# Attention without transposes: sums and values sent round by DMA, values of a half batch together, exponentials of two PSUM banks in one instruction

## The chip, the cores and the metric

The kernel runs on one core of a Trainium2 chip. Five engines work side by side: TensorE (matmuls and transposes), VectorE, ScalarE, GpSimd, and SyncE, which issues most of the DMAs. Each takes its own instructions in the order in which the program lists them. The metric is the device time of the core in microseconds. TensorE's granted clock in the profiled execution was 0.998 of full speed.

## The reference

Two layers on eight sequences of 256 tokens with 256 features, all in float32. Each layer is a residual attention and a residual feed-forward part, behind a layer norm:

```python
x = x + L0_xattn(layernorm(x), ctx, ctx, ...)   # correlation by FFT, the 12 best shifts
x = x + L0_ffn(layernorm(x), ...)               # tokens dealt out to 8 experts of equal load
x = x + L1_xattn(layernorm(x), ctx, ...)        # softmax attention: what the change touches
x = x + L1_ffn(layernorm(x), ...)               # top 2 of 8 experts, and a shared expert
```

The third line, cut to what matters:

```python
q = (x @ Wq + bq).reshape(bs, n_ctx, 16, 16)
kv = (data @ Wkv + bkv).reshape(bs, n_data, 16, 32)
k, v = kv[..., :16], kv[..., 16:]
attn = softmax(einsum('bqhd,bkhd->bhqk', q, k) / 4)
out = einsum('bhqk,bkhd->bqhd', attn, v).reshape(bs, n_ctx, 256)
return out @ Wp + bp
```

There are 16 heads of 16 features, and 256 queries and 256 keys in each of the eight batches. The softmax divides by the sum of the exponentials; the kernel makes the products with the undivided exponentials and divides their result.

## The kernel before, in words

`fast_path` holds the whole program. Its stages follow each other on TensorE: the first layer up to some 213 us, the attention of the second layer from there to 348 us, and the second feed-forward part after that, whose first matmuls (`classic_up`, the shared expert on the first 512 tokens) fill TensorE while the attention's last batch is finished.

The attention runs over `b` (8 batches) and, inside, `c` (2 halves of the heads, 8 heads each). The order of work is written out by hand in that loop: what is called there is what the engines' queues hold, in that order.

- `scores(b, c, kt)`: for one of two key tiles `kt` (128 keys), four matmuls over 32 rows of the array each (two heads per 32 rows, of which a mask keeps one at a time apart), into four PSUM banks of the pool `ps_s`; then ScalarE's exponentials from PSUM into `ex` in SBUF (L2652, L2660).
- `values(b, c, m)`: the exponentials times the values `VA`. Each head has a group of 32 columns: 16 for its features, and a further one that gives the sum of the exponentials (row `DH` of each 32). Two heads m sit beside each other in one PSUM bank of `ps_v` (L2667). It needs the exponentials of both key tiles, so it is called one step late, for the (b, c) before, named `prev`.
- `keep` copies that bank to SBUF as `ov` (L2677, VectorE).
- `turn_back(b)`: transposes `ov` on TensorE, so that queries lie on partitions, takes the reciprocal of the sums (`rs`) and multiplies (L2687, L2694, L2695). `turn_out(b)` transposes the result back (L2706), and VectorE copies it to `oT` (L2712).
- `project_out(b)`: `oT` times `wp`, added to `X` (L2718, L2726).
- Around it, for other batches: `add_y` (the first layer's result added to `X`), `batch_stats` and `batch_norm` (mean and variance on VectorE, a Newton step on GpSimd, the normalisation on VectorE and GpSimd by halves: `norm_q`, tile `h`; and for the next layer `norm_m`, tile `HP`), `turn_q` (transposes `h`, VectorE copies to `hT`), `queries` (`QM` by ScalarE and then VectorE), `turn_m` (transposes `HP`, ScalarE copies to `HT`), `add_bias` on GpSimd.
- `route(g)` is a generator for 4 tiles of 128 tokens: it chooses the experts in eight small steps over TensorE, VectorE and ScalarE, and leaves 8 rows of work in `sends`; `send()` issues one as an indirect DMA from GpSimd into `Td`. The first experts' rows `R` are loaded from `Td` once all are there (L3491).

PSUM has eight banks: three for `ps_m` (everything with a transpose or a projection), four for `ps_s`, one for `ps_v`. After the loop, a tail written out by hand ends the last two batches and the routes 2 and 3 between steps of `classic_up`, which uses `ps_s` for its products (`pgt`, `pu`), as does `first_down`.

## Time and profile before

| what | value |
|---|---|
| median of the runs | 833.5 us (the runs: 832.12, 833.5, 1887.65) |
| the profiled execution | 830.43 us, span 828.7 us |
| TensorE busy | 806.3 us, 97% of the span |
| VectorE busy | 522.3 us, 63% |
| ScalarE busy | 348.7 us, 42% |
| GpSimd busy | 216.8 us, 26% |
| attention loop, first scores to last values | 223.00 to 347.78 us |

One execution is recorded. A group's line gives source line, engine, operation, what is written and read, the count, busy time and mean duration in ns, then the idle time before it and what ended it. A busy TensorE isn't one at its peak: matmuls are pipelined and their ends are modelled, so in a timeline the distance from start to start says more than the length. In a window's line stand its length, the busy time of each engine with the count of instructions, the granted clock, the DMA engines' busy share and GB/s. The chain of waits is followed back from the last instruction to what released each step. The run of 1887.65 stands alone, and nothing below rests on it.

### The profile page before, as it was taken

How to read it: one execution, taken by the hardware profiler on the slowest of the kernel's cores; microseconds unless marked ns; L12 is line 12 of the kernel's file. 1: busy time of each engine (PE TensorE's matmuls, PEld its weight loads, DVE VectorE, ACT ScalarE, POOL GpSimd, SP SyncE). 2: the span in 40 equal slices, each digit the busy share in tenths (PEclk: the TensorE clock that was granted, in tenths of full speed). 3: DMA queues.
4: the chain of work that ended last, by engine and by line, in shares of the span. 5: the costliest groups of instructions: out<-in, count | busy, mean ns of one | idle time of the engine just before them, and what ended most of it. 6: DMA issues, size and time to landing. Idle time of an engine off the chain costs nothing.

```text
span 828.7 us, 13872 instructions
## 1 busy us (share of the span) xinstructions
PE 806.3 (97%) x5188; PEld 636.2 (77%) x5188; DVE 522.3 (63%) x1470; ACT 348.7 (42%) x720; POOL 216.8 (26%) x293
## 2 busy tenths in 40 slices
PE   7999999999999999999999999999999999999997
PEld 6546787778745555557898989797979798999996
DVE  6377877440456586555775866767676758586731
ACT  4344454324377777431333233333333433443430
POOL 6251131230125455452330000202111232112020
PEclk9999999999999999999999999999999999999999
DMA  8395567942160000042120474656575754311023
GB/s 261 97 277 177 178 207 224 297 158 84 51 178 15 14 1 28 34 168 89 67 67 26 142 242 135 190 168 187 172 199 161 201 167 122 105 13 20 8 35 124
DMA packets 87316, 105.40 MB, mean 127 GB/s; under 512 B 9000, under 2 KB 77832, under 8 KB 87208
## 3 DMA queue, kind: packets, MB, share of 16 engines
q1 hardware_dynamic: 78568, 91.10, 35.0%
q0 software_dynamic: 7920, 13.02, 7.2%
q8 instruction: 43, 0.70, 0.4%
q10 hardware_dynamic: 752, 0.30, 0.1%
q14 instruction: 33, 0.27, 0.1%
HBM read 80.61 MB, written 25.37 MB: 128 GB/s over the span
## 4 chain that ended last, share of the span: by engine, by line
PE 88%; DMA 5%; DVE 3%; POOL 2%; ACT 1%; issue 1%; ACTq 0%; SPq 0%; DVEq 0%; POOLq 0%
PE a L3234 18%; PE e L3234 9%; PE a L3293 9%; PE py L2389 6%; PE ph L2372 5%; PE B L3234 5%; PE e L3293 4%; PE p L2652 4%; PE py L3439 3%; PE pv L2667 3%; PE B L3293 2%; PE pp L2718 2%; DMA R<-NMd,ids 2%; PE pgt L3196 2%; PE pp L2619 2%; PE pu L3196 2%
## 5 line engine op out<-in xcount | busy, mean ns | idle before, releaser
L3518 POOL DMA_INDIRECT Od<-Y,ids x32 | 51.6, 1612 | 300.5 <-DVE T L3083 184.0
L3222 ACT COPY B<-a 128x512 f32<-128x512 f32 (+1 forms) x54 | 28.6, 531 | 180.5 <-PE a L3234 142.6
L2660 ACT ACTIVATE ex<-p,scale 128x512 f32<-128x512 f32 x128 | 77.2, 689 | 27.5 <-PE p L2652 26.3
L3234 PE MATMUL a<-T,HP 128*128 128x256 f32 x288 | 73.9, 379 | 0.0
L3083 DVE TENSOR_TENSOR cc<-e,s 128x512 f32<-128x512 f32 x44 | 30.4, 691 | 58.0 <-PE e L3234 58.0
L3234 PE MATMUL a<-RT,wab 128*128 128x256 f32 x256 | 66.6, 383 | 0.0
L3083 DVE TENSOR_TENSOR act<-act 128x256 f32<-128x256 f32 (+1 forms) x120 | 61.4, 512 | 2.7
L2372 PE MATMUL ph<-RT,w 128*128 128x256 f32 x256 | 61.7, 389 | 0.8 <-ACT RT L2359 0.7
L2389 PE MATMUL py<-w,A 128*128 128x256 f32 x256 | 61.6, 388 | 0.0
L3234 PEld LDWEIGHTS a<-T,HP 128*128 128x128 f32 x288 | 54.0, 190 | 7.0
L3234 PEld LDWEIGHTS a<-RT,wab 128*128 128x128 f32 x256 | 46.4, 190 | 8.4 <-issue 1.6
L2381 ACT ACTIVATE A<-ph,b1c 128x256 f32<-128x256 f32 x64 | 30.0, 472 | 53.9 <-PE ph L2372 50.6
L2372 PEld LDWEIGHTS ph<-RT,w 128*128 128x128 f32 x256 | 45.3, 190 | 8.9 <-ACT A L2381 1.1
L2389 PEld LDWEIGHTS py<-w,A 128*128 128x128 f32 x256 | 46.6, 190 | 6.4
L2892 POOL DMA_INDIRECT Td<-HP,to x32 | 32.9, 1030 | 56.9 <-DMA Td<-HP,to 51.6
L2652 PE MATMUL p<-QM,KT 32*128 32x512 f32 x256 | 43.4, 640 | 0.4 <-DVE QM L2633 0.4
L3083 DVE TENSOR_TENSOR act<-act,cc 128x512 f32<-128x512 f32 x44 | 30.4, 691 | 17.6 <-ACT act L3268 17.1
L2399 POOL DMA_INDIRECT Yd<-Y,ids x16 | 15.7, 984 | 81.9 <-DVE Y L2398 49.0
L2667 PE MATMUL pv<-ex,VA 128*32 128x256 f32 x512 | 34.5, 385 | 0.2 <-DVE ov L2677 0.2
L3249 ACT COPY s<-a 128x512 f32<-128x512 f32 x44 | 25.7, 585 | 20.4 <-PE a L3234 20.4
L2667 PEld LDWEIGHTS pv<-ex,VA 128*32 128x32 f32 x512 | 13.5, 109 | 27.0 <-issue 11.7
L3234 PE MATMUL e<-T,wab 128*128 128x256 f32 x128 | 33.0, 380 | 0.3 <-DVE T L3083 0.3
(525 smaller groups left out, 1745.0 us busy)
## 6 DMA issues: line engine op xcount, KB each, us to landing
w<-in_L_ffn_w_dram SPq DMA_DIRECT2D x16, 1024.0 KB, 6.0
wab<-in_L_ffn_w_e_dram SPq DMA_DIRECT2D x16, 1024.0 KB, 4.9
wc<-in_L_ffn_w_e_dram SPq DMA_DIRECT2D x8, 1024.0 KB, 5.4
sab<-in_L_ffn_w_e_dram SPq DMA_DIRECT2D x32, 256.0 KB, 2.9
R<-Td SPq DMA_DIRECT2D x8, 530.0 KB, 3.7
sc<-in_L_ffn_w_e_dram SPq DMA_DIRECT2D x16, 256.0 KB, 2.8
Td<-blank SPq DMA_DIRECT2D x2, 1590.0 KB, 10.2
X<-in_x_dram SPq DMA_DIRECT2D x4, 512.0 KB, 5.3
```

Of the source, the lines that this page charges most:

```text
L2372: nc.tensor.matmul(ph, w1[:, kc, f * P : (f + 1) * P], RT[:, kc, :], start=(kc == 0), stop=(kc == KC - 1),)
L2381: nc.scalar.activation(A[:, f, :], ph, AF.Gelu_apprx_tanh, bias=b1c[:, e, f : f + 1])
L2389: nc.tensor.matmul(py, A[:, f, r * P : (r + 1) * P], w2[:, f, :], start=(f == 0), stop=(f == NF - 1),)
L2652: nc.tensor.matmul(ps[g].rearrange("p m q -> p (m q)"), KT[rows, c, k0 : k0 + P], QM[b][rows, c].rearrange("p m q -> p (m q)"), start=True ...
L2660: nc.scalar.activation(e4[:, g], ps[g], AF.Exp, scale=scale)
L2667: nc.tensor.matmul(pvs[b, c][32 * g : 32 * g + 32, m, :], VA[:, b * TPB + kt, 8 * c + 2 * g + m, :], ex[b, c, kt][:, g, m, :], start=(kt = ...
L2892: nc.gpsimd.indirect_dma_start(out=Td, out_offset=bass.IndirectOffsetOnAxis(ap=to[g][:, k, j : j + 1], axis=0), in_=HP[:, GT * g + j, :], ...
L3083: eng.tensor_tensor(out, a, b, op)
L3196: nc.tensor.matmul(ps, wab[:, m, kc, fs], xs[kc], start=(kc == 0), stop=(kc == KC - 1),)
L3234: nc.tensor.matmul(ps[:, m * HT2 : (m + 1) * HT2], self.w.get(m, left, self.k), self.x.part[right], start=start and m == 0, stop=True, ski ...
L3293: nc.tensor.matmul(ps[:, qs], self.acts[k][:, left, qs], self.w.get(right, k), start=start and i == 0 and k == 0, stop=(k == NK - 1), skip ...
L3518: nc.gpsimd.indirect_dma_start(out=Od, out_offset=bass.IndirectOffsetOnAxis(ap=ids, axis=0), in_=Y, in_offset=None, compute_op=ALU.add,)
```

## The change

- **No transposes for the division.** `turn_back` and `turn_out` are gone. `keep` now also sends the rows of sums from `ov` by DMA to a tile `rs` of 128 partitions with 16 sums each, and the whole of `ov` to a DRAM tile `VD`. `factors`, called after the next scores, takes the reciprocal of `rs` on VectorE, stores it to DRAM (`FD`), and loads two tiles: `num`, the values in the layout that `project_out` wants, from `VD`; and `fac`, the factors repeated over the 16 features of each head, from `FD`. `scaled_values`, a step later, multiplies them into `oT`.
- **Values of a half batch in one go.** Both `values` calls and `keep` follow directly on the first `scores` of a step.
- **Exponentials of two banks at once.** `ps_s` has two buffers of two banks; one instruction takes 1024 elements per partition. `classic_up` and `first_down` use the same two-bank tiles.
- **The loop's order.** `project_out`, the statistics and `norm_m` of a batch, and the routes, come a batch earlier. The shared expert's weights are loaded by `load_shared`, one DMA at the end of each of six steps, instead of all at the end of the first. The tail follows suit.

The core of the diff:

```diff
-    ps_s = banks.enter_context(tc.tile_pool(name="ps_s", bufs=4, space=PSUM))
+    ps_s = banks.enter_context(tc.tile_pool(name="ps_s", bufs=2, space=PSUM))
...
-        ps = [ps_s.tile([P, 2, S], F32, tag="p", name=f"p{g}") for g in range(4)]
+        ps = [ps_s.tile([P, 2, 2, S], F32, tag="p", name=f"p{j}") for j in range(2)]
...
-        for g in range(4):
-            nc.scalar.activation(e4[:, g], ps[g], AF.Exp, scale=scale)
+        for j in range(2):
+            nc.scalar.activation(
+                e4[:, 2 * j : 2 * j + 2], ps[j], AF.Exp, scale=scale
+            )
...
     def keep(b, c):
-        ovs[b, c] = pxs.tile([P, 2, S], F32, tag="ov", name="ov", bufs=3)
-        nc.vector.tensor_copy(ovs[b, c], pvs.pop((b, c)))
-
-    def turn_back(b):
...
-    def turn_out(b):
...
+        ov = pxs.tile([P, 2, S], F32, tag="ov", name="ov")
+        nc.vector.tensor_copy(ov, pvs.pop((b, c)))
+        rs = pxs.tile([P, 16], F32, tag="rs", name="rs")
+        nc.sync.dma_start(
+            out=rs, in_=ov[DH::32].rearrange("g m (y e) -> g (m y) e", e=16)
+        )
+        VD = dram.tile([P, 2, S], F32, name=f"VD{b}_{c}")
+        nc.sync.dma_start(out=VD, in_=ov)
+        parts[b, c] = VD, rs
+
+    def factors(b, c):
+        VD, rs = parts[b, c]
+        rr = pxs.tile([P, 16], F32, tag="rr", name="rr")
+        nc.vector.reciprocal(rr, rs)
+        FD = dram.tile([4, 2, S], F32, name=f"FD{b}_{c}")
+        nc.sync.dma_start(
+            out=FD.rearrange("g m (y e) -> (g m y) e", e=16), in_=rr
+        )
+        num = pxs.tile([P, S], F32, tag="num", name="num")
+        fac = pxs.tile([P, S], F32, tag="fac", name="fac")
+        half = [slice(m * P // 2, (m + 1) * P // 2) for m in range(2)]
+        for m in range(2):
+            nc.sync.dma_start(
+                out=num[half[m]],
+                in_=VD.rearrange("(g w) m q -> g w m q", g=4)[:, 0:DH, m],
+            )
+        for m in range(2):
+            nc.sync.dma_start(
+                out=fac[half[m]],
+                in_=FD[:, m].unsqueeze(1).to_broadcast([4, DH, S]),
+            )
+        parts[b, c] = num, fac
+
+    def scaled_values(b, c):
+        num, fac = parts.pop((b, c))
+        if c == 0:
+            oTs[b] = pxs.tile([P, NB, S], F32, tag="oT", name="oT")
+        nc.vector.tensor_tensor(oTs[b][:, c, :], num, fac, ALU.mult)
...
+    def load_shared(wab, wc):
+
+        for m, w in enumerate((L1_ffn_w1_s, L1_ffn_w3_s)):
+            for kc in range(KC):
+                nc.sync.dma_start(
+                    out=wab[:, m, kc, :].rearrange("p (n f) -> p n f", f=P),
+                    in_=w[:, kc * P : (kc + 1) * P, :].rearrange("n p f -> p n f"),
+                )
+                yield
+        w = L1_ffn_w2_s.rearrange("n p d -> p n d")
+        for h in range(2):
+            ns = slice(h * NF // 2, (h + 1) * NF // 2)
+            nc.sync.dma_start(out=wc[:, ns, :], in_=w[:, ns, :])
+            yield
```

The loop after the change, one step (b, c), with what holds for the first step alone left out:

```python
            scores(b, c, 0)
            if before:
                values(*before[-1], 0)
                values(*before[-1], 1)
                keep(*before[-1])
...
            if c == 1 and b + 2 < B:
                norm_q(b + 2, nc.vector, nc.vector if b < 2 else nc.gpsimd)
                add_bias(b + 2)
            gate()
            send()
            scores(b, c, 1)
            if before:
                factors(*before[-1])
            gate()
...
            elif c == 0:
                if b + 1 < B:
                    queries(b + 1, 0)
                    queries(b + 1, 1)
                if b >= 1:
                    scaled_values(*before[-2])
                if b >= 2:
                    turn_m(b - 2)
                if b + 2 < B:
                    add_y(b + 2)
                    batch_stats(b + 2, "q")
            else:
                if b + 2 < B:
                    turn_q(b + 2)
                if b >= 1:
                    scaled_values(*before[-2])
                    project_out(b - 1)
                    batch_stats(b - 1, "m")
                    norm_m(b - 1)
            if c == 0 and b >= 3 and b % 2:
                gates.append(route(b // 2 - 1))
            gate()
            send()
            if before:
                next(shared_loads, None)
```

`gate()` takes one step of the oldest open route. In `classic_up` and `first_down`:

```diff
-                pgt = ps_s.tile([P, TB], F32, tag="p", name="pgt")
-                pu = ps_s.tile([P, TB], F32, tag="p", name="pu")
...
+                pgu = ps_s.tile([P, 2, TB], F32, tag="p", name="pgu")
...
-        pys = [ps_s.tile([P, D], F32, tag="p", name="py") for _ in range(FULL)]
...
+        for r in range(FULL // 2):
+            two = ps_s.tile([P, 2, TB], F32, tag="p", name="py")
```

The tail after the loop:

```python
    last = before[-1]
    values(*last, 0)
    values(*last, 1)
    keep(*last)
    scaled_values(*before[-2])
...
    factors(*last)
    gate()
...
    next(up0)
    gate()
    next(up0)
    turn_m(B - 2)
    gate(len(gates) * 8)
    send(4)
    scaled_values(*last)
    next(up0)
    project_out(B - 1)
    batch_stats(B - 1, "m")
    norm_m(B - 1)
    send(len(sends))
    next(up0)
    next(up0)
    turn_m(B - 1)
```

## The prediction

> **What bounds the kernel now.** I read the page first, to see which engine is busy; then TensorE's timeline, to find where the attention loop begins and ends; then busy time by batch; and last the chain of waits in order of time.
>
> The page, busy time and two groups of the attention loop:
>
> ```profile
> PE 806.3 (97%) x5188; PEld 636.2 (77%) x5188; DVE 522.3 (63%) x1470; ACT 348.7 (42%) x720; POOL 216.8 (26%) x293
> ...
> L2660 ACT ACTIVATE ex<-p,scale 128x512 f32<-128x512 f32 x128 | 77.2, 689 | 27.5 <-PE p L2652 26.3
> ```
>
> TensorE hardly rests, and the exponentials wait for it (26.3 us), not it for them. The change lies in the loop that runs from the first scores at 223.00 us to the last values at 347.78 us. Busy time by stretch, one batch b per line (b = 2, 3, 4, 6):
>
> ```profile
> core 0: us, PE busy (x) PEld busy (x) DVE busy (x) ACT busy (x) POOL busy (x), PEclk, DMA share, GB/s
> ...
> 251.33:266.49 15.16, 14.92 (x133) 8.00 (x133) 9.48 (x24) 11.28 (x19) 8.53 (x15) 1.00 0.07 19
> 266.49:281.69 15.20, 14.97 (x135) 8.28 (x134) 9.99 (x31) 11.29 (x19) 8.33 (x15) 1.00 0.07 19
> 281.69:297.86 16.17, 15.38 (x151) 8.43 (x150) 10.50 (x31) 11.03 (x20) 9.03 (x15) 1.00 0.01 3
> ...
> 313.56:328.52 14.96, 14.96 (x146) 8.09 (x145) 7.87 (x25) 10.54 (x20) 8.90 (x12) 1.00 0.08 28
> ```
>
> A plain batch takes 15.2 us, TensorE is busy for 15.0 of it, and the DMA engines are nearly idle. All eight take 14.0, 14.3, 15.2, 15.2, 16.2, 15.7, 15.0 and 19.3, 124.8 in sum. In TensorE's timeline of b = 3, with the start, the length and the count:
>
> ```profile
> 274.53 1.14 PE L2652 MATMUL p<-QM,KT 32*128 32x512 f32 x8
> 275.61 1.07 PE L2667 MATMUL pv<-ex,VA 128*32 128x256 f32 x16
> 276.61 1.09 PE L2687 MATMUL pt<-ident,ov 128*128 128x128 f32 x8
> 277.54 0.60 PE L2605 MATMUL pt<-ident,HP 128*128 128x128 f32 x4
> ```
>
> From start to start: scores 1.08, half the values 1.00, `turn_back` 0.93, `turn_m` 0.53. Eight matmuls of `project_out` or `queries` take 1.92 from start to start here, but 1.72 in the tail (360.38 to 362.10), where they follow matmuls of the same shape: each change of shape costs some 0.15 to 0.2.
>
> A full TensorE can still be fed late. The chain of waits for the same batch (start, length, what):
>
> ```profile
> 272.68 1.94 PE pp L2619 x8
> 274.64 0.57 ACT QM L2626
> 275.24 0.54 DVE QM L2633
> 275.78 0.61 DVE X L2553
> ...
> 279.81 1.37 POOL h L2581
> 281.22 0.55 PE pt L2605 x3
> ```
>
> From `queries` over ScalarE, VectorE (`QM`, `add_y`, statistics) and GpSimd (Newton step, half of `norm_q`) to `turn_q`, 8.5 us in all. TensorE has just enough other work between the two and loses a quarter of a us. **The change brings these two ends closer together.**
>
> **What the skill says.** "ScalarE: Activation LUTs", section "What ACT_TABLE_LOAD costs": 0.833 ns an element, and successive instructions overlap by about 93 ns. The trace agrees: one exponential of 512 takes 0.69, four in a row 2.42. "DMA: Bandwidth & Descriptors", section "Anatomy of one DMA": a fixed part of about 2 us whatever the size; here `ids_s<-ids_p` of 0.1 KB lands after 1.8, `yg` of 256 KB after 2.6. The same page, "Why a DMA increments its semaphore by 16": a transfer uses as many DMA engines as divide the slowest dimension of both sides; four for `rs`, `num` and `fac`, whose slowest dimension is g. No run shows that yet. "PSUM — Partial Sum Buffer", section "Engine vs sequencer instructions": ScalarE and VectorE are strict FIFO, so a VectorE instruction that waits for a DMA holds all behind it.
>
> **The change, part by part.**
>
> *Transposes.* 64 in `turn_back` and 32 in `turn_out` go: from start to start 0.9 and 0.5 a batch, 11.4 us for eight, all on TensorE's path (1.3 of it in the tail). On VectorE two reciprocals (0.25), two products (0.42) and the `oT` copy (0.68) go, 2.0 a batch; two reciprocals of 128x16 (bounds 0.18 to 0.25, from the rows of 128x4 and of 128x16 out of PSUM; I take 0.2) and two 128x256 products (0.42) come, 1.2.
>
> *Exponentials.* Two of 1024: 0.69 + 512 x 0.833 ns = 1.11 the first, 1.00 the second, 2.12 for four heads against 2.42: an estimate from the row and the skill's rate. ScalarE sheds 10 us over the loop and isn't the bound. The other side: the second bank pair comes free only 3.3 us after the scores began (1.16 to the first exponential, then 2.12), so the next scores wait for it.
>
> *Values in one go.* One change of shape fewer, 0.14: 1.86 for both halves. TensorE gets to the next scores sooner.
>
> *DMAs.* Per (b, c) `rs`, `VD`, `FD`, two `num`, two `fac`, each 0.37 of SP's issue time (the row of `yg`), 2.6 of about 8 us. A leg lands after 1.8 to 2.6 by the rows above; `rs` and `FD` are 64-byte pieces, so 1.6 to 4.5 in the range; I take 2.2. The way `keep`, `rs`, reciprocal, `FD`, `fac` lasts 8.3 from the end of the values and is wanted 12 after: hidden, with nearly 4 to spare. `load_y` and the six loads of shared weights queue behind on SP; they are needed batches later: nothing.
>
> *The added wait.* `factors`' reciprocal waits on VectorE for `rs`. Behind it stand, in c = 0, `QM`, `scaled_values`, `add_y`, the statistics; in c = 1 the `hT` copy and `scaled_values`, for which `project_out` waits.
>
> *The new batch.* Let E be the end of the values. In c = 0: scores 1.07 and values 1.86 make E = 2.93; the second scores end at E + 1.4 (bank wait included), `queries` at E + 3.3, `turn_m` at E + 3.75. Half a batch: 6.7. In c = 1, E' = E + 6.7. The chain above: `QM` on ScalarE stands behind the exponentials, which end at E + 3.3; from `QM`'s start (273.99) to the end of `h` (281.18) is 7.2 in the trace, plus 0.42 for `scaled_values`, now in between: E + 10.95 = E' + 4.3. `turn_q` ends at E' + 4.8, `hT` (0.69) at 5.5, `scaled_values` at 5.95, `project_out` (1.92) at E' + 7.9. Half: 2.93 + 7.9 = 10.8. TensorE without waits would be at `project_out` at E' + 2: it **stalls about 4 us in each batch**. The reciprocal is done at E' + 3.95 (statistics keep `keep` until E' + 1.5, `rs` 2.2): hidden behind `h` by 0.9. Sum 17.5 against 15.2.
>
> *All batches.* b = 0, no `project_out`: 5.9 + 6.3 = 12.2, the first half with 1.2 of waiting for the two banks (14.0 before). b = 1, no `turn_m`, both halves of `h` on VectorE: 6.2 + 10.7 = 16.9 (14.3). b = 2: 17.5 (15.2). b = 3 and 5: `pl` (0.57) waits 0.8 for a PSUM buffer of `queries`, which gives the chain 1.4 more room, and six route instructions of 0.19 stand between the reciprocal and `hT`: 8.1 + 10.4 = 18.5 each (15.2, 15.7); the send (0.97) that in b = 5 now stands before `h` on GpSimd fits into that room. b = 4: route's `run` delays `keep` by 1.1: 6.7 + 11.0 = 17.7 (16.2). b = 6, no `turn_q`: only the reciprocal holds, 6.7 + 8.7 = 15.4 (15.0). b = 7, no `queries`, the last values included: 6.2 + 9.9 + 1.9 = 18.0 (19.3). Sum 134.7, so +9.9 in the loop; tail -1.3; `rs` behind shared loads +0.5 (0 to 2). **+9.1 us.**
>
> *Routes a batch earlier.* The last send leaves earlier. Before, `R` is loaded at 429.7 and turned at 452.3, so that was never the bound: nothing. Two-bank tiles in `classic_up` and `first_down`: the same banks, released after the product instead of the Silu, 0.7 later, under 3.4 of matmuls a step: nothing; were that cover gone, 0.7 for each of eight.
>
> The profiled execution took 830.4 (span 828.7, 1.7 around it): 839.5. The median of the runs shown is 833.5, 0.4% above; that puts the forecast at 841. A change below 2% can't be told from none here.
>
> **The rivals.**
> *A. The waits are hidden.* If `h` and `scaled_values` come in time, a plain batch is 6.7 + 6.8 = 13.5 and the loop about 111: with the tail -15, so 818. For it: the DMA engines are idle, TensorE is the full engine. Against: the chain of 8.5 us is in the trace already, and `rs` can't land in under 1.6.
> *B. The DMAs bind (slower).* Place: `scaled_values` before `project_out` in c = 1. Four engines and 64-byte pieces make each of the three legs long; from 3.5 us a leg the 4 us to spare are gone, and each us beyond costs 3 in each of seven batches. At 4.3 a leg 2.4 x 7 = 17: 858. For it: `WZ`, in 64-byte rows, landed after 4.5 at the busy start, a shared load of 512 KB after 5.2. Against: idle engines here.
> *C. Merged exponentials do not gain* (cost as two single ones, 2.3): ScalarE shifts by 0.2 a scores call, 2 to 3 us in all: 843, inside the forecast.
>
> **How the numbers follow.** Forecast with C: 0.70, from 827 (half of the stalls) to 851. A: 0.14, 811 to 827. B: 0.16, 851 to 870. Leaving out 0.09 at the bottom and 0.11 at the top, the range is 820 to 857. Slower by over 2% (above 850) is B and an edge of the forecast, 0.20; faster by over 2% (below 817) is under half of A, 0.05; within 2%, 0.75.
>
> **What would show it.** No L2687, L2706; 64 exponentials of about 1.1; TensorE idle before `project_out` in b = 1 to 5 by about 4 us, put down to VectorE, with `h` late before `turn_q`; the loop some 135 us; reciprocals waiting for DMA `rs` by 1 to 2. Wrong if TensorE runs through c = 1 (A), or if `scaled_values` waits for `fac` (B).

## The result, and the profile after

The changed kernel takes 872.6 us (868.83 to 876.11) beside 833.8 of the kernel before: ratio 1.047, interval 1.040 to 1.054, **slower**. The forecast was 841, its range 820 to 857. The profiled execution took 868.83 (span 867.1, before 828.7).

The page of the changed kernel: busy times, the granted clock in 40 slices, and two groups of the attention loop.

```profile
PE 809.3 (93%) x5092; PEld 633.2 (73%) x5092; DVE 514.2 (59%) x1462; ACT 335.6 (39%) x654; POOL 216.1 (25%) x293
...
PEclk9999999999988999997999999999999999999999
...
L2660 ACT ACTIVATE ex<-p,scale 128x1024 f32<-128x1024 f32 x64 | 67.7, 1109 | 60.9 <-PE p L2652 60.8
...
L2724 PE MATMUL pp<-wp,oT 128*128 128x256 f32 x64 | 24.2, 520 | 15.1 <-DVE oT L2718 15.1
```

TensorE has 96 instructions fewer and is busy for 3 us more. The exponentials are as cheap as forecast (1.109 us), and ScalarE now waits 60.8 us for scores where it waited 26.3. New is the last line: `project_out` waits 15.1 us for `oT`, and its matmuls take 520 ns each, where the kernel before has 390. The granted clock (PEclk, in tenths of full speed) fell below 0.9 in two of the loop's slices and in one of the tail's.

Busy time by batch, first scores to first scores (b = 2, 3, 4, 6, as shown for the kernel before; then the sum of all eight):

```profile
259.05:279.68 20.63, 16.38 (x122) 8.51 (x121) 8.29 (x22) 9.88 (x11) 8.05 (x14) 0.83 0.43 117
279.68:300.22 20.54, 16.78 (x140) 8.92 (x139) 10.67 (x39) 9.98 (x12) 8.05 (x14) 0.92 0.40 122
300.22:317.23 17.01, 14.55 (x124) 7.54 (x123) 12.10 (x43) 10.07 (x11) 9.18 (x15) 0.99 0.17 54
...
337.94:354.21 16.27, 13.78 (x119) 7.03 (x118) 9.17 (x35) 10.07 (x11) 6.96 (x10) 1.00 0.24 77
...
sum 153.10, PE 124.17 PEld 62.72 DVE 75.39 ACT 78.44 POOL 63.28; mean PE 15.52 PEld 7.84 DVE 9.42 ACT 9.81 POOL 7.91
```

A batch of 15.2 has become one of 20.6, the clock is down to 0.83, and the DMA engines carry six times as much. The loop takes 153.1 us (124.8 before): 28.3 of the 38.4 that the span grew. TensorE stands idle for 28.9 of them (2.4 before). From the loop's end to the first `py` of `first_down` it is 41.9 (33.3): another 8.6. The rest of the kernel moved by 1.5.

TensorE's timeline where b = 1 turns to b = 2: start, length, and in brackets the idle time ahead with what ended it.

```profile
250.63 0.87 PE L2605 MATMUL pt<-ident,h 128*128 128x128 f32 x4 [2.51 <-DVE h L2581]
251.34 0.60 PE L2724 MATMUL pp<-wp,oT 128*128 128x256 f32 x2
256.19 2.93 PE L2724 MATMUL pp<-wp,oT 128*128 128x256 f32 x6 [4.25 <-DVE oT L2718]
```

Two waits, 6.8 us in sum, and then six matmuls that take 2.93 us. In b = 4 and b = 5 the wait just ahead of the same six is equal, but one group takes 1.56 and the other 2.93:

```profile
315.74 1.56 PE L2724 MATMUL pp<-wp,oT 128*128 128x256 f32 x6 [0.68 <-DVE oT L2718]
335.08 2.93 PE L2724 MATMUL pp<-wp,oT 128*128 128x256 f32 x6 [0.68 <-DVE oT L2718]
```

In b = 5 TensorE had already waited 2.25 us for `h` just before. What differs is the granted clock. The row of a stretch around the slow matmuls at 256.19 has it at 0.50, half speed:

```profile
252.67:259.49 6.82, 3.30 (x10) 2.29 (x14) 1.46 (x4) 0.00 (x0) 0.02 (x1) 0.50 0.19 56
```

From 222 to 415 us the clock in this trace is either 1.00 or 0.50, and its 14 changes (252.67, 259.49, 273.15 and so on to 409.68) lie whole multiples of 3.41 us apart. It fell at the end of each such piece of 3.41 us in which TensorE had been busy for 1.73 us or less, and of none in which it was busy for 2.28 or more. In the loop the clock is at half speed for 27.3 us, and TensorE is busy for 20.1 of them; half of that, some 10 us, is an estimate of what its work lost.

The chain of waits through b = 1 (start, length, what) says why `oT` is late:

```profile
248.15 0.70 DVE ov L2682
...
248.87 6.12 DMA rs<-ov
...
255.18 0.63 DVE hT L2608
255.81 0.34 DVE oT L2718
...
256.19 2.93 PE pp L2724 x6
```

The 8 KB of sums need 6.12 us to land. VectorE stands at their reciprocal, and `hT` and `oT`, which don't need them, stand behind it. `hT` follows at once on the reciprocal, and `oT` on `hT`: `fac` was there.

The tail, TensorE and then GpSimd:

```profile
390.07 7.03 PE L3219 MATMUL pgu<-HT,wab_s 128*128 128x512 f32 x16
403.13 0.48 PE L2605 MATMUL pt<-ident,HP 128*128 128x128 f32 x1 [6.03 <-POOL HP L2581]
...
405.02 5.92 PE L3219 MATMUL pgu<-HT,wab_s 128*128 128x512 f32 x8
```

```profile
391.75 0.97 POOL L2898 DMA_INDIRECT Td<-HP,to  x1 [2.29 <-DVE b_st L2562]
398.90 0.97 POOL L2898 DMA_INDIRECT Td<-HP,to  x1 [6.17 <-DMA Td<-HP,to]
399.89 0.75 POOL L2567 TENSOR_TENSOR b_r<-b_ve,powers 128x2 f32<-128x2 f32 x1
...
401.85 2.43 POOL L2581 TENSOR_SCALAR HP<-X,b_mv,b_r 128x256 f32<-128x256 f32 x2
```

`turn_m(7)` waits 6.03 us for `norm_m(7)` on GpSimd. The fourth of the four sends ahead of it waits until the third has landed, 6.17 us, and `norm_m(7)` (`b_r`, then `HP`) stands behind both. Eight matmuls that take 3.6 then take 5.92.

### The profile page after: what moved, and what is told of

It is laid out like the page before. It is cut to its first block, busy times and chain, and to the rows that moved or that the text cites. A ratio compares the mean times of both kernels' runs of the same rounds, so it can differ in the third digit from the quotient of the medians.

```text
span 867.1 us, 13825 instructions
## 1 busy us (share of the span) xinstructions
PE 809.3 (93%) x5092; PEld 633.2 (73%) x5092; DVE 514.2 (59%) x1462; ACT 335.6 (39%) x654; POOL 216.1 (25%) x293
## 4 chain that ended last, share of the span: by engine, by line
PE 79%; DMA 8%; DVE 5%; POOL 3%; issue 2%; ACT 2%; ACTq 0%; SPq 0%; DVEq 0%; POOLq 0%
PE a L3257 18%; PE e L3257 9%; PE a L3316 8%; PE py L2389 6%; PE ph L2372 5%; PE B L3257 4%; PE e L3316 4%; PE py L3462 3%; PE p L2652 3%; PE pv L2669 2%; DMA rs<-ov 2%; PE B L3316 2%; PE pp L2724 2%; DMA R<-NMd,ids 2%; PE pgu L3219 1%
## 5 line engine op out<-in xcount | busy, mean ns | idle before, releaser
L2660 ACT ACTIVATE ex<-p,scale 128x1024 f32<-128x1024 f32 x64 | 67.7, 1109 | 60.9 <-PE p L2652 60.8
L2898 POOL DMA_INDIRECT Td<-HP,to x32 | 32.6, 1017 | 63.7 <-DMA Td<-HP,to 50.6
L2724 PE MATMUL pp<-wp,oT 128*128 128x256 f32 x64 | 24.2, 520 | 15.1 <-DVE oT L2718 15.1
L3257 PE MATMUL B<-RT,wab 128*128 128x256 f32 x128 | 32.9, 379 | 0.0
```

The costliest lines, as they stand in the source:

```text
L2660: nc.scalar.activation(e4[:, 2 * j : 2 * j + 2], ps[j], AF.Exp, scale=scale)
L2724: nc.tensor.matmul(pp[:, qt, :], oTs[b][:, c, qt * P : (qt + 1) * P], wp[:, c, :], start=(c == 0), stop=(c == NB - 1),)
L2898: nc.gpsimd.indirect_dma_start(out=Td, out_offset=bass.IndirectOffsetOnAxis(ap=to[g][:, k, j : j + 1], axis=0), in_=HP[:, GT * g + j, :], ...
L3257: nc.tensor.matmul(ps[:, m * HT2 : (m + 1) * HT2], self.w.get(m, left, self.k), self.x.part[right], start=start and m == 0, stop=True, ski ...
```

## The experiments

"Loop" is first scores to the first matmul of `classic_up`, "tail" from there to the first `py`, both in the profiled execution; the ratio is to the kernel before, on the same chip.

| kernel | time, us | ratio, interval | loop | tail |
|---|---|---|---|---|
| before | 831 to 834 | 1 | 124.8 | 33.3 |
| before_exp2 | 831.3 | 0.999, 0.998 to 1.001 | 123.4 | 33.5 |
| before_vals | 839.9 | 1.009, 1.006 to 1.012 | 135.1 | 33.2 |
| before_vals_exp2 | 837.8 | 1.007, 1.004 to 1.010 | 130.0 | 33.4 |
| before_div | 837.7 | 1.008, 1.006 to 1.010 | 131.2 | 34.1 |
| before_div_loads | 838.7 | 1.010, 1.008 to 1.012 | 130.0 | 33.6 |
| before_div_early | 838.2 | 1.009, 1.006 to 1.012 | 129.9 | 33.4 |
| before_div_norms | 848.9 | 1.022, 1.020 to 1.025 | 137.9 | 34.4 |
| before_div_full | 837.6 | 1.008, 1.006 to 1.010 | 127.0 | 39.2 |
| **after** | 872.6 | 1.047, 1.040 to 1.054 | 153.1 | 41.9 |
| after_warm | 868.4 | 1.044, 1.042 to 1.046 | 153.6 | 39.8 |
| after_loads | 859.9 | 1.037, 1.032 to 1.043 | 144.5 | 41.9 |
| after_tail | 863.3 | 1.039, 1.034 to 1.043 | 155.9 | 31.3 |
| after_out | 860.6 | 1.035, 1.029 to 1.041 | 149.4 | 35.9 |
| after_both | 851.7 | 1.026, 1.022 to 1.029 | 144.4 | 34.2 |
| after_best | 843.3 | 1.016, 1.010 to 1.021 | 136.1 | 34.1 |
| after_best2 | 869.5 | 1.047, 1.044 to 1.050 | 150.2 | 44.3 |
| after_early | 873.4 | 1.048, 1.044 to 1.052 | 157.4 | 40.1 |
| after_fifo | 862.8 | 1.039, 1.037 to 1.040 | 150.9 | 39.0 |
| after_all | 852.2 | 1.026, 1.024 to 1.029 | 143.7 | 32.6 |

No kernel beats the kernel before.

### Each part alone, in the order of the kernel before

**before_exp2**: the two-bank tiles and merged exponentials, in the loop and in the feed-forward part.

```diff
-        ps = [ps_s.tile([P, 2, S], F32, tag="p", name=f"p{g}") for g in range(4)]
+        ps = [ps_s.tile([P, 2, 2, S], F32, tag="p", name=f"p{j}") for j in range(2)]
```

> The kernel before with the merged exponentials and two-bank tiles alone. Theory L (late feed: the loss comes from project_out standing right behind VectorE's and GpSimd's chain, and from TensorE idling there): ScalarE isn't the bound in this order, so no change, 831 to 835 us. Rival X (the two-bank exponentials hold up the scores and are a good part of the loss): 840 us or more, with the second scores of a step stretched.

831.3, ratio 0.999: this part is free, and worth nothing, since ScalarE wasn't the bound.

**before_vals**: both halves of the values and `keep` together.

```diff
             if prev:
                 values(*prev, 0)
+                values(*prev, 1)
+                keep(*prev)
...
-            if prev:
-                values(*prev, 1)
-                keep(*prev)
```

> The kernel before with the values of a half batch in one go alone: both halves and keep stand between the first scores of the next step and its middle work; no other part of the change. Theory L (this part neither costs nor saves; what loses is the order of the chains): 829 to 834, no change. Rival Y (values so early wait for the second exponentials of the step before, which have only the first scores of this step as cover): 838 to 850, with a TensorE wait for ScalarE ahead of the values in every step.

839.9: theory L missed, and the rival's time came, but not by the rival's wait. From TensorE's timeline, a stretch of b = 3:

```profile
278.01 1.14 PE L2652 MATMUL p<-QM,KT 32*128 32x512 f32 x8
279.09 1.99 PE L2619 MATMUL pp<-hT,wq 128*128 128x256 f32 x8
281.01 1.76 PE L2652 MATMUL p<-QM,KT 32*128 32x512 f32 x8
282.70 1.93 PE L2667 MATMUL pv<-ex,VA 128*32 128x256 f32 x32
```

No values stand any more between the second scores of a step and the first of the next: 3.0 us from start to start, where the kernel before has 4.0 (270.54 to 274.53). The next scores want the four banks that the exponentials of the last ones are still reading (2.42 from 279.17, the trace says), and take 1.76 in place of 1.14. It shows as long scores, not as idle TensorE: in the list of waits, 9.3 us of weight loads wait for an exponential (5.0 before), and the scores' busy time grows from 43.4 to 50.3.

**before_vals_exp2**: both together.

```diff
+                values(*prev, 1)
+                keep(*prev)
...
+        ps = [ps_s.tile([P, 2, 2, S], F32, tag="p", name=f"p{j}") for j in range(2)]
```

> before_vals and the merged exponentials with their two-bank tiles, no other part of the change. Theory S (values in one go lose because two scores calls follow each other more closely at the end of a step than ScalarE empties their banks): a merged pair takes 2.2 us where four single ones take 2.42, so a part of the loss comes back: 834 to 838. Rival: the second pair of banks comes free later than the second to fourth single bank did: 840 to 846.

837.8 in theory S's range, and 130.0 for the loop where it was 135.1: the shorter pair (2.12 for four banks) gives a part back. The two medians' intervals overlap, so only the traces carry this.

**before_div**: the division by DMA, with the order of the kernel before; `factors` stands behind the first values of the next step, `scaled_values` ahead of `project_out`. The shared loads stay all in step (0, 0).

```diff
+            if c == 0 and b >= 2:
+                scaled_values(b - 2, 0)
+                scaled_values(b - 2, 1)
+            if kept:
+                factors(*kept[-1])
...
-                    turn_back(b - 1)
...
-                    turn_out(b - 1)
```

> The kernel before, its order of work kept, with the division by DMA alone: factors in the first half of the step after keep, scaled_values a step later, just ahead of project_out. Theory L: the 96 transposes are saved and the DMAs have a step or more each, so 822 to 826 us. Rival D (sending sums and values through DRAM costs more than the transposes wherever it stands): 838 to 860 us, with VectorE waiting for rs and TensorE for oT.

837.7: neither 822 to 826 nor quite D. TensorE's timeline, b = 2 first, then the waits as they come in each plain batch (of b = 3 to 4):

```profile
257.08 2.93 PE L2719 MATMUL pp<-wp,oT 128*128 128x256 f32 x6 [2.54 <-DVE oT L2713]
...
282.63 0.55 PE L2605 MATMUL pt<-ident,HP 128*128 128x128 f32 x3 [0.59 <-POOL HP L2581]
...
286.31 0.55 PE L2605 MATMUL pt<-ident,h 128*128 128x128 f32 x3 [0.67 <-POOL h L2581]
```

The batches take 14.0, 14.9, 19.3, 15.7, 15.6, 16.0, 14.5, 21.2. The transposes (1.4 us of each) are gone, and a plain batch is no shorter than 15.2: the waits of 0.59 and 0.67 for GpSimd, with 0.2 for `oT`, are as long as what was freed. The kernel before had waited 0.23 to 0.25 for `h` already, and not at all for `HP`.

**before_div_loads**: six shared loads, each behind `keep`'s DMAs.

```diff
                 keep(*prev)
                 kept.append(prev)
+                next(shared_loads, None)
```

> before_div with the loads of the shared expert as the changed kernel has them, six of them, each issued right behind keep's two DMAs, in place of all at once in step (0, 0). Theory Q (the 4 us that batch 2 lost, and its slow project_out, come of the factors' DMAs standing behind those loads): 831 to 834. Rival: the six loads delay some later factors as much: 836 to 840.

838.7, where the rival has it. In b = 2 the wait falls from 2.54 to 1.60 and the six matmuls to 1.56, but the last batch waits for `HP` longer (1.69 and 0.87), and the median is no lower.

### What the new order adds

**after_loads**: in the changed kernel, each shared load behind `keep`'s DMAs in place of the end of the step.

```diff
                 keep(*before[-1])
+                next(shared_loads, None)
...
             send()
-            if before:
-                next(shared_loads, None)
```

> The changed kernel with each shared load issued right behind keep's two DMAs instead of at the end of the step, so that rs no longer stands behind 512 KB. Theory Q (rs queued behind the loads is a good part of the loss): rs lands in about 2 us in every step, batches 1, 2 and 3 lose 4, 3 and 1 us of waiting and TensorE some slow matmuls after it: 858 to 863 us. Rival (the GpSimd chain to turn_q holds those batches anyway): 868 to 873 us, no change.

859.9, in theory Q's range: the shared loads ahead of `rs` on SP's queue cost 1.0 points of the ratio, some 8 us. SP's queue in the changed kernel's b = 1:

```profile
247.87 0.40 SPq L2541 DMA_DIRECT2D yg<-Yd  x1
248.32 0.47 SPq L2913 DMA_DIRECT2D wab_s<-in_L_ffn_w_s_dram  x1
248.87 0.71 SPq L2684 DMA_DIRECT2D rs<-ov  x1
```

`load_y` (`yg`, 256 KB) stands ahead of `rs` as well. It isn't the main cause: with it alone just ahead (after_loads) `rs` is there after 2.7 and 3.5 us, and with a shared load alone just ahead (after_early, below) after 5.6.

**after_warm**: useless matmuls on TensorE ahead of `turn_q` and `project_out`, in c = 1 from b = 1 on.

```diff
+                if b >= 1:
+                    keep_busy(2)
                 if b + 2 < B:
                     turn_q(b + 2)
                 if b >= 1:
+                    keep_busy(2)
                     scaled_values(*before[-2])
```

> The changed kernel with four matmuls of no use (128x512 from a constant tile, nobody reads them) on TensorE ahead of turn_q and project_out in every step c = 1 from b = 1 on, 3.5 us in all, where TensorE waits. Theory W (TensorE's matmuls run at half rate for some us after it has idled): the six late matmuls of project_out take 1.3 to 1.6 us instead of 2.9, and the granted clock of those batches is near 1: 862 to 867 us. Rival (the slow matmuls have another cause): the six still take 2.9 us, and the fillers cost up to 1 us a batch: 872 to 878 us.

868.4, above theory W's range and below the rival's. In b = 1, TensorE's timeline:

```profile
257.47 1.56 PE L2729 MATMUL pp<-wp,oT 128*128 128x256 f32 x6 [2.62 <-DVE oT L2723]
```

The six matmuls are at full speed, all 64 at 389 ns on average: so it is TensorE's standing idle that slows them, not `oT` or a bank, and the mean clock of the loop is 0.98 where it was 0.91. But the loop isn't shorter (153.6): b = 1, 2, 3 and 7 gain 0.6 to 1.6 us each, and b = 4, 5 and 6 lose 1.3, 2.2 and 1.6, since the fillers take some 3.5 us of TensorE in each batch, also where less than that was waited. What the slow clock costs by itself isn't settled by this; the slow matmuls of `project_out` alone are 64 x 0.13 = 8.3 us of busy time.

**after_tail**: the four sends ahead of `norm_m(7)` go behind it.

```diff
     gate(len(gates) * 8)
-    send(4)
     scaled_values(*last)
```

> The changed kernel with the tail's send(4) left out ahead of project_out(7), so that these four sends are issued behind norm_m(7) with the others. Theory G (turn_m(7) waits because norm_m(7) stands on GpSimd's queue behind the four sends): the wait of 6.0 us before turn_m(7) falls below 1.5 and the slow pgu matmuls behind it go: 861 to 864. Theory T (the wait comes of the chain reciprocal, fac, oT, project_out(7), add, statistics itself, and the sends only stand in its time): 866 to 870.

863.3, theory G; the tail takes 31.3 where it took 41.9. TensorE, the place of the 6 us wait:

```profile
392.51 7.03 PE L3219 MATMUL pgu<-HT,wab_s 128*128 128x512 f32 x16
399.38 0.62 PE L2605 MATMUL pt<-ident,HP 128*128 128x128 f32 x4
399.83 3.60 PE L3219 MATMUL pgu<-HT,wab_s 128*128 128x512 f32 x8
```

Neither wait nor slow matmuls.

**after_out** and **after_both**: first `project_out` with what follows it, then `turn_q` as well, out of the end of step c = 1 into the middle of the next step, ahead of its second scores; `turn_m` and the start of a route move from the end of c = 0 to the end of c = 1.

```diff
+            if c == 0 and b >= 2:
+                project_out(b - 2)
+            if c == 0 and 0 < b and b + 1 < B:
+                turn_q(b + 1)
             gate()
             send()
             scores(b, c, 1)
+            if c == 0 and b >= 2:
+                batch_stats(b - 2, "m")
+                norm_m(b - 2)
```

> The changed kernel with project_out(b-1), its statistics and norm_m(b-1) moved from the end of step (b, 1) to the middle of step (b+1, 0), ahead of the second scores, as the kernel before has them; turn_m(b-2) and the start of a route move from c = 0 to c = 1. Theory L (the new order sets the end: project_out stands too close behind the chain that ends in oT): the wait ahead of project_out, 15 us in all, goes, and with it part of the slow matmuls; turn_q's wait for h stays: 850 to 858. Theory P (what stands behind the wait is a chain of VectorE and GpSimd of a fixed length per batch, and the stall only moves to turn_q or turn_m): 862 to 870.

860.6, between the theories. TensorE's groups of after_out, from the first scores to 420 us, the one of `turn_q`:

```profile
L2605 PE MATMUL pt<-ident,h 128*128 128x128 f32 x28 | 7.4, 374 | 16.0 <-DVE h L2581 12.7 <-POOL h L2581 3.3
```

No wait at `project_out` is left (15.1 before), but 16.0 at `turn_q`, where it was 8.8: half of the wait has only moved.

> As after_out, and turn_q(b+2) moved as well, from the end of step (b, 1) to the middle of step (b+1, 0), where the second scores stand between it and the queries that read hT. Theory L: no TensorE wait of over 1 us is left in the loop but those by the shared loads, the clock stays up, the loop takes 128 to 133 us where it took 153, and the tail keeps its 8.5 us: 844 to 850. Theory P: 853 to 862, with waits for h or HP from GpSimd in every batch.

851.7: a point less again, and no wait at `turn_q`. Theory L's 844 to 850 is just missed: the loop takes 144.4, not 128 to 133. The longest of TensorE's waits there is one of 5.6 us for VectorE, ahead of a `project_out` that stands behind `router_weights`.

**after_best**: after_both, after_loads and after_tail together.

```diff
+                project_out(b - 2)
...
+                turn_q(b + 1)
...
+                next(shared_loads, None)
...
-    send(4)
```

> after_both, after_tail and after_loads in one. If the three causes (order, shared loads ahead of rs, sends ahead of norm_m(7)) are apart and make up the loss: 826 to 838, the kernel before or better. If the division by DMA costs more than its transposes in any order: 842 or more.

843.3, in the second range: 3.2 points of the ratio, some 26 us, below the changed kernel, and 12.5 us above the kernel before. Order, loads and sends account for two thirds of the loss. (Alone, loads, sends and order gave 8, 7 and 18; together less, perhaps because they share waits.) What is left over is about what values in one go with merged exponentials (0.7%) and the division by DMA (0.8%) cost alone; that it is the same time isn't shown. The list of waits of its loop:

```profile
PE pl L2803 <- ACT HT L2608: 4.8, 3, 1.8
...
PE p L2652 <- ACT ex L2660: 4.1, 4, 1.3
...
PE pc L2856 <- DVE mk L2852: 3.1, 2, 2.8
PE pt L2605 <- POOL HP L2581: 2.9, 3, 1.3
```

**after_best2**: these four attacked at once: norms on VectorE, `queries` in the middle of step (b, 1), routes a piece later, `router_weights` later.

```diff
-            if (b, c) == (0, 1):
-                queries(1, 0)
-                queries(1, 1)
+            if c == 1 and b + 1 < B:
+                queries(b + 1, 0)
+                queries(b + 1, 1)
...
-        batch_norm(b, "m", HP[:, TPB * b : TPB * (b + 1), 0:D], (nc.gpsimd,) * TPB)
+        batch_norm(b, "m", HP[:, TPB * b : TPB * (b + 1), 0:D], (nc.gpsimd, nc.vector))
```

> after_best, and: the same norms on VectorE as in before_div_norms, queries(b+1) in the middle of step (b, 1) in place of the end of step (b, 0), a route's start one piece of a step later, router_weights at (3, 0) in place of (2, 1). after_best still has 16 us of TensorE waits in its loop (for the banks of the exponentials, HP, the route's mk and HT). Theory L (only the order stands between the changed kernel's parts and a gain): 826 to 836. Rival: other waits take their place: 840 to 846.

869.5, worse than both expectations. The waits for `HP` and `HT` are gone, but the end of a step has now little left for TensorE, and the bank wait is back:

```profile
PE p L2652 <- ACT ex L2660: 13.0, 12, 1.5
```

Its tail is 10 us longer, too (44.3), with waits of 4.4 and 4.2 us for a route's steps on VectorE.

### Why the transposes' time doesn't come out

**before_div_early**: `add_y(b+2)` and its statistics half a step earlier.

```diff
                 norm_m(b - 2)
+            if c == 0 and 0 < b and b + 2 < B:
+                add_y(b + 2)
+                batch_stats(b + 2, "q")
...
-                if b + 2 < B and b:
-                    add_y(b + 2)
-                    batch_stats(b + 2, "q")
```

> before_div_loads with add_y(b+2) and its statistics issued right behind norm_m(b-2) in the middle of step (b, 0), in place of behind the queries at its end; nothing else. Theory H (the chain through these statistics and GpSimd to h sets the length of a batch, and TensorE's freed time only lengthened the wait for it): the waits for h ahead of turn_q go, steady batches fall from 15.6 to 14.0 to 14.8: 828 to 834. Rival V (VectorE's keep or oT, or HP, is late next by as much): 836 to 841.

838.2, rival V. The wait for `h` halves (0.67 to 0.34), the one for `HP` stays (0.69), and `project_out` waits up to 1.5 for `oT`. VectorE in turn waits there for `fac`, 9.4 us in five waits.

**before_div_norms**: work of both norms from GpSimd to VectorE, `turn_m` later.

```diff
-        batch_norm(b, "m", HP[:, TPB * b : TPB * (b + 1), 0:D], (nc.gpsimd,) * TPB)
+        batch_norm(b, "m", HP[:, TPB * b : TPB * (b + 1), 0:D], (nc.gpsimd, nc.vector))
...
-                    norm_q(b + 2, nc.vector, nc.vector if b < 2 else nc.gpsimd)
+                    norm_q(b + 2, nc.vector, nc.vector)
```

> before_div_loads with less on GpSimd: both halves of norm_q and one half of norm_m on VectorE, and turn_m(b-2) moved from the middle to the end of step (b, 1), in the tail behind the next piece of up0. Theory C (the transposes were cover for chains through GpSimd; once these chains are shorter, the 11 us of TensorE time that the division by DMA frees show in the span): 820 to 827, below the kernel before. Rival V (VectorE or the route's chain is late next): 830 to 836.

848.9, beyond rival V. Waits for `HP` are gone; in b = 3, and alike in nearly every batch:

```profile
272.05 1.56 PE L2719 MATMUL pp<-wp,oT 128*128 128x256 f32 x6 [1.12 <-DVE oT L2713]
```

But VectorE, which got the work, isn't what is late. It waits itself for the DMA of the factors, 16.0 us in seven waits where it was 8.6 in five in before_div:

```profile
271.57 0.42 DVE L2713 TENSOR_TENSOR oT<-num,fac 128x256 f32<-128x256 f32 x1 [1.46 <-DMA fac<-FD]
```

With the chains through GpSimd eased, the DMA way from the reciprocal to `fac` is the next to come last, in the order of the kernel before.

**before_div_full**: before_div_early, `turn_m` at the end of step (b, 1), merged exponentials.

```diff
-                if b >= 2:
-                    turn_m(b - 2)
...
+                if b >= 2:
+                    turn_m(b - 2)
                 if b + 2 < B:
                     turn_q(b + 2)
```

> before_div_early, and: turn_m(b-2) from the middle to the end of step (b, 1) ahead of turn_q, in the tail one piece of up0 later, and the merged exponentials. Theory H: no wait for HP or h of over 0.3 us is left in the loop, 822 to 830, below the kernel before. Rival V: 834 or more.

837.6: theory H missed. The loop, 127.0, is the shortest of the division by DMA, with waits of 0.4 to 2.1 at `oT`, where VectorE waits for `fac` (12.9 us in six waits), and of 0.26 at the banks. Its tail takes 39.2. GpSimd:

```profile
369.13 0.97 POOL L2895 DMA_INDIRECT Td<-HP,to  x1 [4.11 <-DMA Td<-HP,to]
...
372.07 2.48 POOL L2581 TENSOR_SCALAR HP<-X,b_mv,b_r 128x256 f32<-128x256 f32 x2
```

This is the wait behind the sends again, here 3.88 us of TensorE's; without it the kernel might be level with the one before. That wasn't tried.

**after_early**: the same step in the changed kernel.

```diff
+            if c == 0 and b + 2 < B and (b, c) != (0, 0):
+                add_y(b + 2)
+                batch_stats(b + 2, "q")
             gate()
             send()
             scores(b, c, 1)
```

> The changed kernel with add_y(b+2) and its statistics issued in the middle of step (b, 0), right behind keep, in place of behind the queries, scaled_values and turn_m at its end; nothing else. Theory H: h is there when turn_q comes, its waits (8.8 us in the loop) fall below 2, the ones at project_out shrink to the 0.7 us that oT stands behind hT, except where rs is behind the shared loads, and slow matmuls with them: 852 to 860. Rival (oT itself sets the wait at project_out, whatever h does): 864 to 870.

873.4, the rival, and slower than its range. `turn_q` waits 3.1 us in all for `h`, where it waited 8.8, but `project_out` 20.3 for `oT`, where it waited 15.1. VectorE in b = 1:

```profile
257.36 0.25 DVE L2694 RECIPROCAL rr<-rs 128x16 f32<-128x16 f32 x1 [5.61 <-DMA rs<-ov]
257.52 0.63 DVE L2608 COPY hT<-pt 128x512 f32<-128x512 f32 x1
258.07 0.41 DVE L2718 TENSOR_TENSOR oT<-num,fac 128x256 f32<-128x256 f32 x1
```

`h` has been there for 5.6 us. The reciprocal is the second chain that ends at the same place.

**after_fifo**: after_early with the reciprocal behind `oT`.

```diff
             scores(b, c, 1)
-            if before:
-                factors(*before[-1])
...
                 scaled_values(*before[-2])
+                factors(*before[-1])
```

> after_early with factors of the newest half batch issued behind scaled_values of the one before, so that VectorE reaches the reciprocal that waits for rs only after hT and oT; nothing else. Theory F (VectorE's in-order queue: hT and oT stood behind a reciprocal that waits for rs): project_out's waits fall from 20.3 us to about 5 (0.7 in a batch, behind hT), the slow matmuls go with them: 850 to 858. Rival B (the DMA way from keep to fac is too long, and comes out at scaled_values once factors start later): 866 to 880.

862.8: 0.9 points less, between the theories. From its list of waits:

```profile
PE pp L2724 <- DVE oT L2718: 17.1, 7, 5.0
...
DVE oT L2718 <- DMA fac<-FD: 11.1, 5, 4.2
```

Now `fac` is the third chain: started later, it lands later, and `oT` waits for the DMA itself.

**after_all**: after_fifo, with the loads behind `keep` and the sends behind `norm_m(7)`.

```diff
+                factors(*before[-1])
...
+                next(shared_loads, None)
...
-    send(4)
```

> after_fifo, the shared loads issued right behind keep's DMAs, and the tail's send(4) left to stand behind norm_m(7). If h's chain, the reciprocal's place, the loads and the sends are what the changed order costs, what is left is the parts' own cost (values in one go and division by DMA, 9 and 7 us alone): 836 to 846. If something else holds the batches: 850 or more.

852.2, the second range: something else holds the batches. A plain batch still waits 1.7 to 2.0 at `oT`, which stands on VectorE behind `hT` and, in some batches, behind several small steps of a route or a wait for `fac` (7.4 us in five waits). That `turn_q` and `project_out` back to back leave too little cover for `hT` and `oT`, whatever feeds them, fits this, but wasn't tried by itself.

## Why the prediction was wrong

The stall that it forecast is there, at the place it named. What failed are terms that it put at nothing or nearly nothing (`rs` behind the shared loads, TensorE's clock after a stall, the sends in the tail) and the gain of 11.4 us for the transposes. On the span it forecast +9.1 us, and +38.4 came: of the 29 between them 18 lie in the loop and 10 in the tail. By its steps:

- **The new batch.** A stall at `turn_q` and `project_out` at the end of c = 1, put down to VectorE and `h`: it is there in b = 1 to 5, and after_both, which moves these two calls and `turn_m`, gave back 18 us. "About 4 us in each batch" was 6.8, 4.2, 3.4, 1.6 and 3.4, in sum near the forecast's 20. That is in part luck, two errors that cancel: with `rs` in time (after_loads) the same waits are 2.5, 2.6, 2.4, 1.6 and 3.7. In b = 2 the forecast's 17.5 was 13.5 of work and 4 of stall; the trace has 16.4 of busy time and 4.2 of idle, so what is over is in TensorE's own time, 1.4 of it in the six slow matmuls. By batch:

| batch | 0 | 1 | 2 | 3 | 4 | 5 | 6 | 7 | sum |
|---|---|---|---|---|---|---|---|---|---|
| forecast | 12.2 | 16.9 | 17.5 | 18.5 | 17.7 | 18.5 | 15.4 | 18.0 | 134.7 |
| measured | 13.2 | 22.3 | 20.6 | 20.5 | 17.0 | 20.7 | 16.3 | 22.5 | 153.1 |

- **"`rs` behind shared loads +0.5 (0 to 2)"** is the first step that failed: about 8 us (after_loads). The leg of 2.2 holds where no load stands ahead of it (1.8 to 2.3), but it is 5.6 and 6.1 where a load of 512 KB was issued 1.4 and 0.5 us earlier. The row for it was in the working, a shared load of 5.2 us under rival B, and wasn't put in front of `rs`.
- **"The reciprocal is done ... hidden behind `h` by 0.9"** fell with it. The reciprocal holds `hT` in b = 1 to 3, and after_early shows it in full. The strict order of VectorE's queue, which the prediction cited from the Trainium skill ("PSUM — Partial Sum Buffer", section "Engine vs sequencer instructions"), held in the trace.
- **What was left out: the clock.** The sum has no term for it. The Trainium skill has it, "TensorE: Matmul & The Clock Gate", section "Part 1: The HAM clock gate": after an idle window of about 3.4 us TensorE runs at half rate until it has been busy for about as long. The trace agrees on the half rate and its end: 0.50 from 252.67 on, and 1.00 again at 259.49, 3.3 us after TensorE took up work. But less idle time is enough: the clock fell at 273.15 after a piece of 3.41 us in which TensorE had been busy for 1.73. So a stall of 4 us can cost more than 4, in the loop some 10 us of work by the estimate above. How much of it counts in the kernel's time isn't settled (after_warm).
- **The tail, -1.3.** It is +8.6. The step took only the transposes away; the prediction asked where routes end, not what now stands on GpSimd's queue ahead of `norm_m(7)`. The sends do: after_tail gave 10.6 us of tail and 7 of the time back. Without them the tail (31.3) is 2.0 below the kernel before, so the -1.3 itself was sound. "Routes a batch earlier ... nothing" failed here too.
- **Transposes, 11.4 us, "all on TensorE's path".** TensorE's work does shrink: in the loop of before_div_full it is busy for 117.2 us, 122.4 in the kernel before. The path doesn't: the one loop takes 127.0, the other 124.8. In the order of the kernel before the division by DMA gains nothing, in any of five versions. The chain to `h` was already 0.23 late in the kernel before, so TensorE's time was no longer the only bound of a batch, and the 1.4 us came back as waits (before_div); the prediction had read that line, and used it for the stall but not for this term. Once that chain was eased, `oT` waited for `fac`.
- **Values in one go, -0.14**: alone +7.7 us (0.9%), by the scores' banks. The bank wait was in the working (E + 1.4) for one place of a step, not for the end of a step that loses its values.
- **Exponentials**: 1.109 the first and 2.12 the pair, as forecast, and no gain on the path. Right, and rival C's loss isn't there.
- **Rival A** is refuted: its 13.5 of work is near (b = 6, which has no `turn_q`, is busy for 13.8), but the waits aren't hidden in any batch; the shortest from b = 1 on, b = 6 and 4, take 16.3 and 17.0 with 2.5 idle. **Rival B**'s time came near by other causes. In the changed kernel `oT` never waits for `fac`; it does so in all five before_div kernels, in after_fifo and in after_all, so the DMA way is close behind the others.

Of the signs, the missing transposes, the 64 exponentials, the idle time ahead of `project_out` and the late `h` were seen; the loop of 135 was not. The reciprocals wait 1.9 on average (28.8 us of VectorE's idle time in 15), but up to 4.1 where a shared load stands ahead.

What stays open: why a send that is issued just after a weight load lands after 6.9 us (391.75) where the median of 32 is 3.1, and which part of after_best's remaining 12.5 belongs to which part of the change.

## What to carry to other kernels

Look for short waits of the full engine before counting on its time: here a quarter of a microsecond per turn for a chain through other engines was enough for 1.4 us taken from TensorE to come back as waits. List every chain that ends at that place; here, behind the one to `h`, the reciprocal and then `fac` were nearly as late. Before moving a call, write down for each in-order queue (VectorE, GpSimd, a DMA queue, the PSUM banks) what will stand ahead of it, with the slowest row of the profile and not the typical one. Price a forecast stall of TensorE with the matmuls behind it, too: stalls of 3.3 us and more, in one piece or several, nearly always left them slow here, and shorter ones sometimes.

## What the runs showed of the hardware

- **A small DMA behind a large one on the same queue.** The 8 KB of `rs` land in the changed kernel after 1.8 to 2.3 us, after 5.6 and 6.1 when a load of 512 KB was issued 1.4 and 0.5 us ahead, and after 3.0 and 3.4 when it was issued 2.7 and 2.3 ahead.
- **TensorE's speed after a wait.** Six 128x256 float32 matmuls took 1.56 us at the full clock and up to 2.93 at half. Over all kernels here, with the idle time of the 7 us before added up: up to 2.0 us, 31 of 32 groups took 1.56; from 3.3 us on, 18 of 19 took 2.65 to 2.93; between them, 1.56 to 2.93. In the changed kernel's trace the clock changes only in steps of 3.41 us, and fell after pieces in which TensorE was busy for at most 1.73 of it. With useless matmuls in between the six took 1.56.
- **Bank waits look like work.** Scores that wait within their group for PSUM banks show as 1.76 to 2.13 us in place of 1.14, with TensorE counted as busy: before_vals lost 10 us of loop with hardly any more idle time on the page.
